# More result and row buffers for the expert tiles behind the last convolution, in the convolutions' room

## The chip, the core and the metric

The kernel runs on one core of a Trainium2 chip. The metric is the device time of one execution in microseconds (us). Before the change it is 3072.74 us, the median of ten runs (3070.18 to 3075.74).

The core's engines each work through their own list of instructions in order: PE (matrix products), ACT (activations and copies), DVE (elementwise work and reductions), POOL (GpSimd, which here issues the indirect DMAs too) and SP, which issues most of the other DMAs. Engines wait for each other through semaphores. In the profile, "idle before <- X" names what ended an idle time.

## The reference

A layer of 32 small convolution paths is followed by an attention layer without a softmax and a mixture of experts: each of the 25088 tokens goes to the two best of eight experts, and the weighted results are added to it.

```python
x = conv_paths(x)                    # 32 paths 256 -> 4 -> 3x3 -> 4 -> 256, summed, plus x
t = x.reshape(8, 3136, 256)
t = t + attn(layernorm(t))           # per head: q @ (k^T v / N), k and v normalised per head
t = t + moe(layernorm(t))
# moe(tokens), top 2 of 8 experts, weights normalised:
out = tokens
for e in range(8):
    h = gelu(tokens @ w1[e] + b1[e])
    out = out + combine[:, e:e+1] * (h @ w2[e] + b2[e])
```

## The kernel before

**Chunks and slots.** The tokens are cut into 56 chunks of 448 (`S = 56`, seven to an image). The loop over `s` (L1574) goes through 65 slots. In slot `s` the third convolution of chunk `s` is worked, with earlier steps of chunks `s + 1` and `s + 2`, the end of chunk `s - 1`, and attention and routing of chunk `s - 8`. Convolution work ends in slot 56. From slot 57 on (`S + 1`) only attention, routing and expert tiles are left; this is the tail, and the list `apart` is filled there, which makes some helpers choose other layouts (one PSUM bank for each half, an own `index` tile).

**Routing.** Once a chunk's two experts are known, POOL scatters its rows (`pay`, 259 numbers: 256 values, two weights and the token's number) into two DRAM tables, `regions`, by indirect DMA (L1191, eight for each chunk). `pay` has three buffers.

**Expert tiles.** Sorted rows are worked in 210 tiles of 256 rows (`N_ALL`), numbered in the order they are worked. `moe_steps` (L1505) is a hand-made pipeline of five steps for each tile number `n`:

- `tile_in(n)`: PE transposes the rows, ACT copies them to `eT`, DVE copies the token numbers to `index`
- `tile_mid(n - 1, ...)`: first product and GELU to `hT`, in two halves
- `take_rows(n + 2)` and `take_weights(n + 1)`: SP loads the 259 KB of rows and the 513 KB of the expert's weights
- `tile_out(n - 2, ...)`: second product; ACT scales the result by the gate into `y` (L1471), in two halves
- `tile_add()`: POOL adds one half of a finished `y` to the output in DRAM by indirect DMA (L1485)

Before the change `rows` has seven buffers, the weights `w` four and `y` four. A `y` buffer is free when the adds of the tile four back have landed.

**Order of the sums.** The two experts of a token must not be added at the same time. `ordered_sum` (L1493) therefore lets the adds of one block (a routing round `b` and a place `k` of the top two) wait until all adds of the block before have landed. Blocks begin at tiles 130, 137, 144, 149, 154, 158, 162, 165, 168, 172, 176 and 193, among others. The last round is known only when the last chunk is scattered; its tiles are 176 to 209.

**Who sets the order.** PE, ACT and DVE work in the order written out by hand (`places`, L614, and the sort in `issue`, L1536). POOL and SP take their DMAs in the order that the build gives. DMAs of POOL take turns on eight semaphores (lanes), and each one waits until the eighth before it has landed; SP's DMAs have lanes in the same way.

**Room.** `xtp`, `taps`, `split` and `hlp` (L95 to L98) hold the convolutions' tiles. They stay open to the end of the kernel, though nothing uses them in the tail.

Of the kernel before, what the change touches and what calls it, by code (L numbers as in the profile page):

```python
# [8 lines left out]
F32 = mybir.dt.float32  # L9
# [16 lines left out]
def kernel(  # L26
# [25 lines left out]
    B, N, C = x.shape  # L52
# [6 lines left out]
    P = 128  # L59
# [32 lines left out]
            tc.add_manual_dep(ins, halved[0].name, SYNC, reason="not needed by the first chunk")  # L92
        xs_in[s] = X

    xtp = ctx.enter_context(tc.tile_pool(name="xtp", bufs=4))  # L95
    taps = ctx.enter_context(tc.tile_pool(name="taps", bufs=1))
    split = ctx.enter_context(tc.tile_pool(name="split", bufs=1))
    hlp = ctx.enter_context(tc.tile_pool(name="hlp", bufs=2))  # L98
    setup_pool = tc.tile_pool(name="setup", bufs=1)
    setup = setup_pool.__enter__()  # L100

# [155 lines left out]
    def is_chunk(s):  # L257
        return 0 <= s < S
# [198 lines left out]
    slots = ctx.enter_context(tc.tile_pool(name="slots", bufs=4))  # L457
    work = ctx.enter_context(tc.tile_pool(name="work", bufs=2))
# [42 lines left out]
    ROW = C + 3  # L501
    WROW = 2 * NF * C + NF
# [101 lines left out]
    def unordered(ins, group, keep=()):  # L604

        tc.declare_no_dep(ins, group=group, keep=keep, reason="other rows")
# [85 lines left out]
    def conv3_steps(s):  # L692
        steps = []
        units = NF * NQ
        for step in range(0, 4 * units, 2):
            if is_chunk(s):
                steps.append((places["conv3"][0], lambda step=step: (pair(s, step), pair(s, step + 1))))
            if step == 0 and is_chunk(s - 1):
                steps.append((places["conv3"][1], lambda: sum_paths(s - 1, units - 1)))
            if step and step % 4 == 0 and is_chunk(s):  # L700
                steps.append((places["conv3"][1], lambda step=step: sum_paths(s, step // 4 - 1)))
        return steps
# [644 lines left out]
        return [(1.0, fn) for fn in (counts, runs, members, first_rows, experts, rest)]  # L1347


    got, weights_of, turned, hidden, ready = {}, {}, {}, {}, []  # L1350
    landed = set()

    def entry(i, j, most):

        place, own, k, partial, b = slot_of[i]
        loads, (value,) = nc.values_load_multi_w_load_instructions(
            place[0:1, j : j + 1], engines=[mybir.EngineType.SP],
            min_val=0, max_val=most,
            skip_runtime_bounds_check_because="a tile's row and expert, made on the chip",
        )  # L1360
        if b not in landed:
            landed.add(b)
            for ins in before[b]:
                tc.add_manual_dep(loads[0].ins, ins.name, SYNC, reason="rows of the tiles")
        return value
# [11 lines left out]

    def take_rows(i):
        row = entry(i, 0, E * CAPR - TR)
        z = slots.tile([P, 2, ROW], F32, tag="rows", name=f"rows_{i}", bufs=7)  # L1380
        region = regions[slot_of[i][2]]
        ins = nc.sync.dma_start(
            out=z, in_=region[bass.ds(row, TR), :].rearrange("(h p) c -> p h c", p=P)
        ).ins
        unordered(ins, "rows")
        tc.add_to_no_dep_group("tiles", ins)
        got[i] = z

    def take_weights(i):
        e = entry(i, 1, E - 1)  # L1390
        w = slots.tile([P, WROW], F32, tag="w", name=f"w_{i}")
        nc.sync.dma_start(
            out=w, in_=Wd[bass.ds(e, 1), :, :].rearrange("e p c -> (e p) c")
        )
        weights_of[i] = w
# [29 lines left out]
    apart = []  # L1425

    def bank_of(i, h, name):

        if h == 0:
            n = 1 if apart else 2  # L1430
            v = ps_mm.tile([P, n, 256], F32, tag="mm", name=f"{name}_{i}")
            hidden[i, name] = v
        elif apart:
            v = ps_mm.tile([P, 1, 256], F32, tag="mm", name=f"{name}_{i}_{h}")
        else:
            v = hidden[i, name]
        return v[:, h % v.shape[1], :]
# [17 lines left out]
    def tile_out(i, h):  # L1455
        w = weights_of[i]
        eT, g, _ = turned[i]
        if h == 0:
            hidden[i].append(work.tile([P, 2, C], F32, tag="y", name=f"y_{i}", bufs=4))
        hT, y = hidden[i]  # L1460
        own = slot_of[i][1]
        ps = bank_of(i, h, "py")
        nc.tensor.matmul(  # L1463
            ps, own.to_broadcast([P, P]), b2hl, start=True, stop=False
        )
        for f in range(NF):
            nc.tensor.matmul(  # L1467
                ps, hT[:, f, h * P : (h + 1) * P], w[:, (NF + f) * C : (NF + f + 1) * C],
                start=False, stop=(f == NF - 1),
            )  # L1470
        nc.scalar.activation(y[:, h, :], ps, AF.Identity, scale=g[:, h : h + 1])  # L1471
        ready.append((i, h))
# [53 lines left out]
    def at(name, steps):  # L1526

        out, last = [], 0.0
        for place, (_, fn) in zip(places[name], steps, strict=True):
            last = max(last, place)  # L1530
            out.append((last, last, [(0.0, fn)]))
        return out
# [32 lines left out]
    def put_off(m):  # L1565

        return m % NCH == NCH - 1 and m + 1 + A < S
# [6 lines left out]
    for s in range(S + A + 1):  # L1574
        a = s - A
        work_of = []
        era = " alone" if s < A else ""
        if s <= S:
            work_of.append((0.0, 1.0 if is_chunk(s) else 0.1, conv3_steps(s)))
        if is_chunk(s + 2):  # L1580
            work_of.extend(at("conv1" + era, conv1_steps(s + 2)))
        if is_chunk(s + 1):
            work_of.extend(at("taps" + era, [(0.0, lambda: spread_taps(s + 1))]))
            work_of.extend(at("conv2" + era, conv2_steps(s + 1)))
        if is_chunk(s - 1):
            if s < S:
                work_of.extend(at("end" + era, end_steps(s - 1)))
            else:
                work_of.append((0.12, 0.99, end_steps(s - 1)))
        if is_chunk(a + 1):  # L1590
            work_of.extend(at("fetch", [(0.0, lambda: fetch(a + 1))]))
        if is_chunk(a):
            opens = a % NCH == 0
            if opens:
                work_of.extend(at("image", image_steps(a // NCH)))
            if a + A > S:
                work_of.extend(at("attention first last" if opens else "attention last", attn_steps(a)))
            else:
                work_of.extend(at("attention first" if opens else "attention", attn_steps(a)))
        work_of.extend(left)  # L1600
        left = []
        group = waiting
        if waiting and put_off(waiting[0]):
            group = [] if waiting[0] == a - 1 else waiting[:1]
        if group and (len(group) == 2 or group[-1] % NCH == NCH - 1):
            last_image = group[-1] >= S - NCH
            compute, scatters = route_steps(group)
            rt = places["route" if s < S else "route last"]
            work_of.append((rt[0], rt[1], compute))
            if last_image:  # L1610
                work_of.append((places["scatter last"][0], 0.995, sum(scatters, [])))
            else:
                work_of.append((places["scatter"][0], 0.995, scatters[0]))
                left = [(0.0, places["scatter"][1], steps) for steps in scatters[1:]]
            if group[-1] in closing:
                work_of.append((places["plan"][0], places["plan"][1], plan_steps(closing.index(group[-1]))))
            waiting = waiting[len(group) :]
        while r + 1 < len(closing) and known_in[r + 1] <= s:
            r += 1
        if r >= 0 and r + 1 < len(closing):  # L1620
            goal = upto + (known_after[r] - 2 - upto) // (known_in[r + 1] - s)
            if r + 2 < len(closing):
                goal = min(known_after[r] - 2, goal if s < known_in[1] else tiles_by(s))
            work_of.append((places["tiles"][s <= known_in[r]], places["tiles"][2], moe_steps(upto, goal)))
            upto = goal
        if s == 1:
            center_router()
        if 1 <= s <= E:
            work_of.append((0.5, 0.5, [(0.0, lambda: copy_weights(s - 1))]))
            work_of.append((0.8, 0.8, [(0.0, lambda: empty_rows(s - 1))]))  # L1630
        if s == S + 1:
            apart.append(s)
        issue(*work_of)
        if is_chunk(a):
            waiting.append(a)
# [60 lines left out]
```

## Time and profile before

| what | value |
|---|---|
| median of ten runs | 3072.74 us |
| profiled execution | 3079.18 us |
| its span, first to last instruction | 3077.3 us |
| mean granted TensorE clock | 0.965 |
| PE busy over the span | 2850.1 us (93%) |
| POOL busy over the span | 1798.7 us (58%) |
| POOL, adds to the output (L1485), 420 of them | 408.1 us (258) and 250.9 us (162) |
| POOL, scatters (L1191), 448 of them | 428.1 us |

The shares of busy time are means over stages with different limits. The change acts in the last tenth of the span alone, so this part is read by itself. There the slices of 50 us show:

| slice (us) | PE busy | POOL busy | granted clock | DMA share |
|---|---|---|---|---|
| 2700 to 2750 | 45.43 | 34.27 | 0.93 | 1.01 |
| 2750 to 2800 | 39.10 | 37.92 | 0.83 | 0.84 |
| 2800 to 2850 | 45.00 | 36.57 | 0.93 | 0.95 |
| 2850 to 2900 | 39.77 | 37.59 | 0.86 | 0.83 |
| 2900 to 2950 | 44.59 | 30.21 | 0.97 | 0.92 |
| 2950 to 3000 | 47.48 | 41.76 | 1.00 | 0.95 |
| 3000 to 3050 | 50.00 | 39.23 | 1.00 | 0.94 |

"DMA share" is the mean busy share of the core's 16 DMA engines. POOL's busy time counts the making of an indirect DMA, not the 0.30 us between two of them, in which the next is issued.

### The profile page before, as it was taken

The page shows a single profiled execution, that of the slowest core. Times are in us where ns is not written, and L with a number is a line of the kernel's source. Part 1 is how long each engine was busy: PE and PEld are TensorE (multiplying, and loading weights), DVE is VectorE, ACT ScalarE, POOL GpSimd, SP SyncE. Part 2 cuts the span into 40 slices and gives each one's busy share as a digit, 9 for nine tenths or more (in the row PEclk, how much of TensorE's full clock was granted, in tenths as well). Part 3 has the DMA queues.
Part 4 walks back from the last instruction along what each step waited for, and adds up shares of the span by engine and source line. Part 5 has one row for each costly group of instructions (what it writes and reads, how often), then busy time and mean ns, then how long its engine had stood idle before and what let it go on. Part 6 is the DMA issues. An engine that isn't in the chain of part 4 may idle for free.

```text
span 3077.3 us, 54367 instructions
## 1 busy us (share of the span) xinstructions
PE 2850.1 (93%) x16901; PEld 1659.1 (54%) x16901; DVE 2144.8 (70%) x5705; ACT 1915.2 (62%) x3859; POOL 1798.7 (58%) x1333
## 2 busy tenths in 40 slices
PE   7999888888899999999999999999999997998898
PEld 3334444334455555555555555555555555787687
DVE  6877887888777877787877877787778775443100
ACT  4666566556566676667766766667666664554355
POOL 2332345444465766757666666676664656677677
PEclk9999899989899999999999999999999998998999
DMA  3555444436477777677777767778877766998897
GB/s 103 148 115 133 119 138 132 132 100 185 111 181 183 181 202 202 164 199 188 202 189 176 202 177 193 194 178 205 193 168 181 190 168 149 229 278 214 201 221 172
DMA packets 373233, 538.19 MB, mean 175 GB/s; under 512 B 91488, under 2 KB 283344, under 8 KB 372944
## 3 DMA queue, kind: packets, MB, share of 16 engines
q1 hardware_dynamic: 289984, 430.49, 48.7%
q0 software_dynamic: 82368, 103.47, 20.0%
q8 instruction: 135, 2.21, 0.3%
q14 instruction: 154, 1.26, 0.2%
q10 hardware_dynamic: 592, 0.76, 0.1%
HBM read 248.42 MB, written 192.75 MB: 143 GB/s over the span
## 4 chain that ended last, share of the span: by engine, by line
PE 54%; DVE 6%; DMA 4%; ACT 4%; POOL 3%; issue 3%; POOLq 0%; ACTq 0%; DVEq 0%; SPq 0%
PE ph L1447 11%; PE c L660 9%; PE py L1467 9%; PE su L681 8%; PE te L1403 3%; DMA out_dram<-y,index 3%; PE at L1010 2%; PE py L1463 2%; PE kv L837 2%; PE c L324 2%; DVE r L668 2%; ACT r L665 2%; POOL hsd L801 2%; PE at L1006 1%; PE c L288 1%
## 5 line engine op out<-in xcount | busy, mean ns | idle before, releaser
L668 DVE SCALAR_TENSOR_TENSOR r<-c,nb,r 128x448 f32<-128x448 f32 x1792 | 1127.2, 676 | 380.0 <-ACT r L665 375.3
L665 ACT ACTIVATE r<-c,b3t 128x448 f32<-128x448 f32 x1792 | 1036.9, 634 | 342.3 <-PE c L660 336.0
L660 PE MATMUL c<-hl,W3hl 64*128 64x448 f32 x3584 | 701.2, 430 | 36.1 <-ACT r L665 19.1
L1191 POOL DMA_INDIRECT regions<-pay,rrowi x448 | 428.1, 956 | 304.9 <-PE c L660 178.2
L660 PEld LDWEIGHTS c<-hl,W3hl 64*128 64x128 f32 x3584 | 331.9, 189 | 488.1 <-issue 216.6
L1485 POOL DMA_INDIRECT out_dram<-y,rows x258 | 408.1, 1582 | 319.4 <-ACT y L1471 241.5
L681 PE MATMUL su<-r,gather 128*32 128x448 f32 x3584 | 538.7, 565 | 44.3 <-DVE r L668 34.4
L1471 ACT ACTIVATE y<-py,rows 128x256 f32<-128x256 f32 x420 | 195.7, 473 | 467.4 <-PE py L1467 340.0
L1447 PE MATMUL ph<-eT,w 128*128 128x256 f32 x1680 | 458.5, 405 | 16.8 <-ACT hT L1451 7.9
L1467 PE MATMUL py<-w,hT 128*128 128x256 f32 x1680 | 434.9, 384 | 0.0
L1447 PEld LDWEIGHTS ph<-eT,w 128*128 128x128 f32 x1680 | 303.7, 197 | 147.0 <-ACT hT L1451 29.3
L801 POOL TENSOR_TENSOR hsd<-hsd,half 112x36 f32<-112x36 f32 x49 | 302.4, 6172 | 98.0 <-DVE hsd L799 95.2
L754 POOL TENSOR_TENSOR norm<-t,hmean 112x512 f32<-112x512 f32 x112 | 115.5, 1057 | 356.1 <-DVE hmean L743 242.8
L1467 PEld LDWEIGHTS py<-w,hT 128*128 128x128 f32 x1680 | 293.9, 193 | 27.1
L1485 POOL DMA_INDIRECT out_dram<-y,index x162 | 250.9, 1549 | 94.5 <-issue 27.1
L1451 ACT ACTIVATE hT<-ph,w 128x256 f32<-128x256 f32 x420 | 197.2, 478 | 166.6 <-PE ph L1447 111.5
L681 PEld LDWEIGHTS su<-r,gather 128*32 128x32 f32 x3584 | 99.1, 109 | 231.2 <-DVE r L668 105.8
L1463 PE MATMUL py<-b2hl,own 128*128 128x256 f32 x420 | 176.6, 421 | 17.3 <-ACT y L1471 8.3
L1015 DVE SCALAR_TENSOR_TENSOR X<-at,rs,X 112x256 f32<-112x256 f32 x224 | 106.7, 476 | 99.7 <-PE at L1010 98.8
L1463 PEld LDWEIGHTS py<-b2hl,own 128*128 128x128 f32 x420 | 80.8, 192 | 145.9 <-issue 49.1
L324 PE MATMUL c<-R,W2t 96*32 96x448 f32 x1344 | 152.3, 556 | 2.5 <-ACT r L665 2.4
L1403 PE MATMUL te<-ident,rows 128*128 128x128 f32 x840 | 136.3, 286 | 19.6 <-ACT y L1471 18.6
(267 smaller groups left out, 3282.6 us busy)
## 6 DMA issues: line engine op xcount, KB each, us to landing
w<-Wd SPq DMA_DIRECT2D x210, 513.0 KB
rows<-regions SPq DMA_DIRECT2D x210, 259.0 KB
xi<-in_x_dram SPq DMA_DIRECT2D x56, 448.0 KB
hl<-hi SPq DMA_DIRECT2D x112, 224.0 KB
tTs<-xT SPq DMA_DIRECT2D x56, 448.0 KB
ts<-t SPq DMA_DIRECT2D x56, 448.0 KB
tT<-tTs SPq DMA_DIRECT2D x56, 448.0 KB
X<-ts SPq DMA_DIRECT2D x56, 448.0 KB
```

Of the source, the lines that this page charges most:

```text
L324: nc.tensor.matmul(ps[0][32 * g : 32 * g + 32, :CH], W2t[:, g, dy, :], R[:, g, :].rearrange("q (r w) -> q r w", w=W58)[:, dy : dy + ROWS, ...
L660: product = nc.tensor.matmul(tiles[g][:, :CH], W3hl[rows, ab, cg, :], hl[rows, ab, :], start=True, stop=True)
L665: nc.scalar.activation(r, tiles[0][:, :CH], AF.Relu, bias=b3t[:, cg, 2 * ab : 2 * ab + 1])
L668: nc.vector.scalar_tensor_tensor(r, tiles[1][:, :CH], nb3[:, cg, 2 * ab + 1 : 2 * ab + 2], r, op0=ALU.max, op1=ALU.add,)
L681: nc.tensor.matmul(ps[32 * c4 : 32 * c4 + 32, :CH], gather, unit.pop((s, 4 * u + c4)), start=(ab == 0), stop=(ab == NQ - 1),)
L801: nc.gpsimd.tensor_tensor(sd, sd, half[:T, :].rearrange("q (k h) -> q k h", k=KT), ALU.pow)
L1191: ins = nc.gpsimd.indirect_dma_start(out=regions[n], out_offset=bass.IndirectOffsetOnAxis(ap=v["row_i"][:, (m - group[0]) * KT + k, n : n ...
L1403: nc.tensor.transpose(tp[:, f, h * P : (h + 1) * P], z[:, h, f * P : (f + 1) * P], ident)
L1447: nc.tensor.matmul(ps, w[:, f * C + hf * P : f * C + (hf + 1) * P], eT[:, f, :], start=(f == 0), stop=(f == NF - 1),)
L1463: nc.tensor.matmul(ps, own.to_broadcast([P, P]), b2hl, start=True, stop=False)
L1467: nc.tensor.matmul(ps, hT[:, f, h * P : (h + 1) * P], w[:, (NF + f) * C : (NF + f + 1) * C], start=False, stop=(f == NF - 1),)
L1485: ins = nc.gpsimd.indirect_dma_start(out=out_rows, out_offset=at, in_=y[:, h, :], in_offset=None, compute_op=ALU.add, **partial,).ins
```

## The change

The four pools of the convolutions are placed on the right side of SBUF and closed at slot `S + 1`; a pool `late` is opened in their room. A helper `buffer` chooses for each tile number, from slot 57 on, between the old buffers of a tag and the new ones, in a fixed turn: of twelve tiles in a row four take the old `y` buffers and eight the new ones; of eleven, seven take the old `rows` buffers and four the new. The weights go through the same helper with no new buffers. Nothing that is computed changes, nor what is loaded, scattered or added.

```diff
-    xtp = ctx.enter_context(tc.tile_pool(name="xtp", bufs=4))
-    taps = ctx.enter_context(tc.tile_pool(name="taps", bufs=1))
-    split = ctx.enter_context(tc.tile_pool(name="split", bufs=1))
-    hlp = ctx.enter_context(tc.tile_pool(name="hlp", bufs=2))
+    conv_pools = [
+        tc.tile_pool(name=name, bufs=bufs, side="right")
+        for name, bufs in (("xtp", 4), ("taps", 1), ("split", 1), ("hlp", 2))
+    ]
+    xtp, taps, split, hlp = (p.__enter__() for p in conv_pools)
...
+    more = {}
+    first_late = []
+
+    def buffer(i, pool, tag, bufs, shape):
+
+        if apart and not first_late:
+            first_late.append(i)
+        if apart and more[tag] and (i - first_late[0]) % (bufs + more[tag]) >= bufs:
+            return apart[0].tile(shape, F32, tag=tag, name=f"{tag}_{i}", bufs=more[tag])
+        return pool.tile(shape, F32, tag=tag, name=f"{tag}_{i}", bufs=bufs)
...
-        z = slots.tile([P, 2, ROW], F32, tag="rows", name=f"rows_{i}", bufs=7)
+        z = buffer(i, slots, "rows", 7, [P, 2, ROW])
...
-        w = slots.tile([P, WROW], F32, tag="w", name=f"w_{i}")
+        w = buffer(i, slots, "w", 4, [P, WROW])
...
-            hidden[i].append(work.tile([P, 2, C], F32, tag="y", name=f"y_{i}", bufs=4))
+            hidden[i].append(buffer(i, work, "y", 4, [P, 2, C]))
...
         if s == S + 1:
-            apart.append(s)
+            for pool in reversed(conv_pools):
+                pool.__exit__(None, None, None)
+            more.update(y=8, rows=4, w=0)
+            apart.append(
+                ctx.enter_context(tc.tile_pool(name="late", bufs=1, side="right"))
+            )
```

## The prediction, made before the changed kernel was run

> **What bounds the kernel now.** I read the waits by engine first. Up to 2714 us ACT never waits for a result buffer; from there to the end one wait leads all others on ACT. It is the wait for a `y` buffer, held until the adds of the tile four back have landed:
>
> ```profile
> ACT y L1471 <- DMA out_dram<-y,index: 116.8, 28, 11.6
> ```
>
> That looks like what the change is for. Second view: the timeline of POOL, which issues these adds (L1485) and the scatters of routed rows (L1191), each an indirect DMA.
>
> ```profile
> 2738.15 1.54 POOL L1485 DMA_INDIRECT out_dram<-y,index  x1 [0.30 <-issue]
> 2740.00 1.54 POOL L1485 DMA_INDIRECT out_dram<-y,index  x1 [0.30 <-ACT X L1053]
> 2749.34 1.54 POOL L1485 DMA_INDIRECT out_dram<-y,index  x1 [7.80 <-ACT lg L1019]
> 2751.19 1.54 POOL L1485 DMA_INDIRECT out_dram<-y,index  x1 [0.30 <-issue]
> 2753.03 1.54 POOL L1485 DMA_INDIRECT out_dram<-y,index  x1 [0.30 <-issue]
> 2754.88 1.54 POOL L1485 DMA_INDIRECT out_dram<-y,index  x1 [0.31 <-issue]
> 2756.73 0.97 POOL L1191 DMA_INDIRECT regions<-pay,rrowi  x1 [0.30 <-DVE rs L1025]
> 2758.01 0.96 POOL L1191 DMA_INDIRECT regions<-pay,rrowi  x1 [0.30 <-issue]
> ```
>
> An add takes 1.85 us of POOL (1.54 and 0.30 between), a scatter 1.25, back to back; it is so from 2688.36 to 3071.81, but for eight stops. The stop of 7.80 is put down to ACT, yet that `y` had long been written. Pairing ACT's `y` writes with POOL's adds in their order, tile 144, whose add opens here, was ready at 2736.11. The wait is the order of the sums: tile 144 is the first of a new block, and its add waits until all adds of the block before have landed. I call such a stop a drain.
>
> The same pairing over tiles 136 to 209 shows every half ready at least 0.53 us before its add starts (least at tile 207, 3060.49 against 3061.02), most 28.61 us before (tile 147). So POOL never waits for `y` in these 383 us: POOL is the bound, and PE and ACT wait for POOL. Its time is summed by the groups of POOL from 2689 on:
>
> ```profile
> L1485 POOL DMA_INDIRECT out_dram<-y,index x150 | 232.4, 1549 | 84.0 <-issue 26.5 <-ACT y L1471 21.9 <-ACT lg L1019 11.5
> L1191 POOL DMA_INDIRECT regions<-pay,rrowi x56 | 53.1, 948 | 17.1 <-issue 13.7 <-DMA regions<-pay,rrowi 1.2 <-DVE index L1413 0.6
> ```
>
> Busy 232.4 + 53.1 = 285.5, idle 84.0 + 17.1 = 101.1, together 386.6. Of the idle, 37.9 are the eight drains (7.80, 3.12, 4.74, 3.25, 6.52, 4.41, 4.88, 3.14), 3.15 the wait before tile 135 at 2688 (PE was late there), and 60 the 0.30 between 197 instructions. The change touches neither the busy time nor the 0.30. Only the drains are left to move.
>
> Third view: the stretches of the drains, whose last two columns are the share of the DMA engines and GB/s.
>
> ```profile
> 2741.60:2749.30 7.70, 7.70 (x46) 6.96 (x45) 3.22 (x18) 4.08 (x9) 0.00 (x0) 1.00 1.09 307
> 2787.80:2790.90 3.10, 3.10 (x12) 2.72 (x11) 0.81 (x2) 0.88 (x3) 0.00 (x1) 0.50 0.37 42
> 2809.20:2813.80 4.60, 4.60 (x40) 4.01 (x39) 1.65 (x12) 3.52 (x10) 0.00 (x0) 1.00 1.08 263
> 2884.80:2888.00 3.20, 3.20 (x11) 2.64 (x11) 0.50 (x4) 1.44 (x4) 0.00 (x0) 0.63 0.40 47
> 2898.80:2905.30 6.50, 6.36 (x34) 5.30 (x34) 0.34 (x2) 2.81 (x8) 0.00 (x1) 1.00 0.92 272
> 2919.80:2924.20 4.40, 4.40 (x26) 3.92 (x25) 0.30 (x2) 1.62 (x5) 0.01 (x1) 1.00 1.04 262
> 2938.70:2943.50 4.80, 4.80 (x27) 4.25 (x26) 0.23 (x2) 2.31 (x7) 0.00 (x0) 1.00 0.87 209
> 3006.10:3009.20 3.10, 3.10 (x20) 2.74 (x18) 0.30 (x2) 1.75 (x4) 0.00 (x1) 1.00 0.57 148
> ```
>
> A drain is as long as the adds take to land. With the DMA engines at 0.87 to 1.09 it lasts 4.4 to 7.8 us; at 0.37 and 0.40 it lasts 3.1 and 3.2. These two are quiet because PE had just stood still for a `y` buffer, and the weights, which come when PE has finished the tile four back, stood still with it. SP's timeline shows the pause:
>
> ```profile
> 2778.70 0.38 SPq L1382 DMA_DIRECT2D rows<-regions  x1
> ...
> 2786.02 0.47 ACT L1471 ACTIVATE y<-py,rows 128x256 f32<-128x256 f32 x1 [11.61 <-DMA out_dram<-y,index]
> ...
> 2791.96 0.33 SPq L1392 DMA_DIRECT2D w<-Wd  x1
> ```
>
> **The change part by part.** *Room and order.* Moving the four convolution pools to the other side changes addresses; the built program has the same instructions in the same order on all five engines. No wait differs before tile 127, and nothing can differ in time before 2714, where the first `y` wait ends late. Cost 0; no cover is needed.
>
> *Eight more `y` buffers.* A tile's `y` now waits for the adds of the tile twelve back. The 116.8 us of ACT's waits go, and with them most of the PE idle they make: in 50 us slices from 2700 to 3000 PE is idle 4.57 + 10.90 + 5.00 + 10.23 + 5.41 + 2.52 = 38.6 us. What is late next is POOL, with the same 206 instructions: gain on the path 0. PE runs up to twelve tiles ahead, until a later round's rows are not scattered yet (POOL's own scatters, last at 2876) or its work is done, and the last adds drain as now.
>
> PE ahead pulls loads forward: 513 KB of weights and 259 KB of rows a tile, for eight tiles 6.2 MB. At 286 GB/s (2700 to 2750) that is 22 us of DMA, where the three slices from 2700 to 2850 leave 150 - 50 x (1.01 + 0.84 + 0.95) = 10. So the engines stay full through the drain at 2787, and nothing pauses the loads at 2884. I price both at the mean of the five drains over 0.87: (7.80 + 4.74 + 6.52 + 4.41 + 4.88) / 5 = 5.67. That adds 5.67 - 3.12 + 5.67 - 3.25 = +5.0 us. The other six are taken as they are. Bounds for all eight: at 7.80 each 62.4 - 37.9 = +24.5; at 3.12 each 25.0 - 37.9 = -12.9, if the loads have gone ahead and leave the engines free.
>
> *Four more `rows` buffers.* From 2714 SP waits 10.5 us for ACT before issuing rows, six times; these waits go. Behind them in SP's queue stand the weights, which wait 156.7 us for PE by themselves, and PE waits nowhere for rows landing between 2700 and 3000. Cost 0, covered by the weights' wait; without that cover the rows come at most 10.5 us earlier, off POOL's path.
>
> *Waits that become explicit.* `pay` (L1046) waits for the scatters three chunks back, so far covered by the `y` waits; behind it on ACT stand `y`, `eT` and `hT`, and PE waits for these. At tile 153 it needs scatters issued by 2769; ACT was there at 2799 and would have to be over 20 us earlier to feel it. Were it felt, PE loses lead, not POOL: 0. POOL's lanes also wait for the eighth DMA back (10.6 us in the scatter stretches), and stay 0.30 apart throughout: 0, inside the upper bound if landings pass that.
>
> **Sum.** 0 + 5.0 + 0 + 0. The profiled execution took 3079.18 (span 3077.3), 6.4 above the median, so it would take 3084.2; on the median, 3072.74 + 5.0 = **3077.7 us**.
>
> The Trainium skill (Perfetto Trace Analysis, Optimization Strategy) says that consistent bubbles on the engine that should be saturated can mean too little SBUF for the next tile. The row above has such bubbles, 28 of them, but on ACT and PE, while POOL is the saturated one; by the rule the sum would be 3072.74 - 38.6 = 3034, by the row 3077.7. Against the change speaks DMA: Bandwidth & Descriptors (Issuing engines are not separate DMA queues): DMAs of all issuers run on the same 16 engines and interleave, as the drains' lengths against the engines' share agree.
>
> **The rivals.**
> *Slower.* Earlier loads keep the engines full from 2714 to 2850, and the landings there go to the longest seen: 2787 and 2809 last 7.80, 2884 and 3006 the loaded mean 5.67. 4.68 + 3.06 + 2.42 + 2.53 = +12.7, 3085.4. It decides once the eight drains gain 6.15 us together. For it: 1.09 at the 7.80 drain, and only 10 us of free DMA. Against it: the drain at 2809 lasted 4.74 at 1.08. Bound 3097.
> *Faster.* Loads are the same in number, so what comes early is missing later; drains fall to 3.12, -12.9, 3059.8. Against it: PE will still work its 4.13 us a tile through the late drains. A full gain of PE's idle (3034) would need POOL to wait for `y`, and it does not.
> *The change does nothing.* If the buffers never get ahead: 3072.7. Against it: the built program drops the waits.
>
> **How the numbers follow.** Within 0.2% (6.15 us, about what a measurement of this kernel can tell) hold the forecast (0.40) and the idle change (0.10): 0.50. Slower by more, the first rival and the forecast's upper side: 0.34. Faster by more: 0.16, of it 0.03 for the full gain. The drains' bounds give 3059.8 to 3097; I cut the upper end where about 0.06 is left: 3060 to 3090, below it 0.08.
>
> **What would show it.** Right: ACT's wait for `out_dram` almost gone, PE done tens of us before POOL, POOL's adds still 1.85 apart to the end, `y` ready long before its add, the drains at 2787 and 2884 with the engines near 1. Wrong: a POOL stop outside the block borders, drains that sum far from 43 us, or POOL clearly off 386.6 - 37.9 = 348.7 us outside them.

## The result, and the profile after

| | before | after |
|---|---|---|
| median of the runs of this comparison | 3073.62 us (28 runs) | 3084.06 us (8 runs) |
| ratio, 95% interval | | 1.0036, 1.0027 to 1.0045 |
| profiled execution / its span | 3079.18 / 3077.3 us | 3087.18 / 3085.2 us |
| mean granted TensorE clock | 0.965 | 0.963 |
| last matrix product of PE ends | 3066.6 us | 3040.7 us |
| from the start of tile 135's add to the end of the last add | 383.44 us | 393.39 us |

The kernel became 10.4 us slower. ACT and PE did what more result buffers are for: ACT's wait for `y`, 116.8 us before, is almost gone, and PE is done 25.9 us earlier than before. The waits by engine, from 2714 us on (us in total, times, longest); ACT first, then PE:

```profile
ACT y L1483 <- DMA out_dram<-y,index: 6.2, 6, 2.4
```

```profile
PE te L1415 <- DMA rows<-regions: 25.9, 1, 25.9
```

The second row is PE's lead running out once, up to 2857 us: it has run up to tiles whose rows POOL has not yet scattered. POOL did not become faster. The groups of POOL from 2686 us on (busy us, mean ns of one, idle before):

```profile
L1497 POOL DMA_INDIRECT out_dram<-y,index x150 | 232.4, 1550 | 92.2 <-ACT y L1483 27.2 <-issue 22.6 <-ACT hT L1463 15.8
L1192 POOL DMA_INDIRECT regions<-pay,rrowi x56 | 54.9, 980 | 17.1 <-issue 15.5 <-DMA regions<-pay,rrowi 0.6 <-DVE full_i L1255 0.3
```

The adds (now L1497) are as many and as long as before, the scatters (L1192) cost 1.8 us more. What grew is the idle time before the adds, 84.0 to 92.2, though an add's `y` now lies ready far earlier. POOL's timeline shows where, at the first of the eight drains (start, length, and in brackets the idle time before):

```profile
2736.05 1.54 POOL L1497 DMA_INDIRECT out_dram<-y,index  x1 [0.30 <-ACT eT L1419]
2737.89 1.54 POOL L1497 DMA_INDIRECT out_dram<-y,index  x1 [0.30 <-ACT hT L1463]
2746.20 1.54 POOL L1497 DMA_INDIRECT out_dram<-y,index  x1 [6.76 <-DVE X L1016]
2748.05 1.54 POOL L1497 DMA_INDIRECT out_dram<-y,index  x1 [0.30 <-ACT hT L1463]
```

Taken from the start of tile 135's add, the 393.39 us are 287.31 busy, 60.09 in the 0.30 between instructions, and 46.00 in eight drains; before it was 285.52, 60.07 and 37.86. There is no other stop of POOL in either. Of the 9.95 us, 8.14 lie in the drains and 1.79 in POOL's own instructions. (The profiled executions differ by 8.00 us, since the one of after came to tile 135 some 2 us earlier, where nothing can differ yet.) The drains one by one, by the tile that opens the block:

| tile | 144 | 149 | 154 | 165 | 168 | 172 | 176 | 193 | sum |
|---|---|---|---|---|---|---|---|---|---|
| before | 7.80 | 3.12 | 4.74 | 3.25 | 6.52 | 4.41 | 4.88 | 3.14 | 37.86 |
| after | 6.76 | 4.86 | 5.45 | 5.47 | 5.09 | 7.08 | 6.18 | 5.11 | 46.00 |

The stretches of the after kernel's drains (length; busy time and count on PE, its weight loads, DVE, ACT and POOL; clock; share of the DMA engines, the packets' times added up, which can pass 1; GB/s):

```profile
2739.40:2746.20 6.80, 6.80 (x43) 6.15 (x42) 2.32 (x9) 3.68 (x9) 0.04 (x2) 1.00 1.07 281
2784.70:2789.50 4.80, 4.80 (x42) 4.36 (x40) 2.06 (x14) 2.98 (x8) 0.00 (x0) 1.00 1.08 290
2807.70:2813.10 5.40, 1.86 (x17) 1.38 (x16) 4.29 (x26) 3.77 (x10) 0.04 (x1) 1.00 1.00 264
2885.90:2891.30 5.40, 5.40 (x32) 4.79 (x31) 0.17 (x1) 3.23 (x8) 0.00 (x0) 1.00 0.92 259
2902.10:2907.20 5.10, 5.10 (x29) 4.49 (x28) 0.30 (x2) 2.95 (x7) 0.02 (x1) 1.00 1.04 267
2921.70:2928.80 7.10, 7.10 (x40) 6.30 (x39) 0.60 (x4) 4.43 (x9) 0.03 (x1) 1.00 0.94 254
2943.30:2949.40 6.10, 6.10 (x35) 5.40 (x34) 0.30 (x2) 3.94 (x8) 0.00 (x0) 1.00 0.89 256
3012.00:3017.10 5.10, 5.10 (x28) 4.53 (x28) 0.30 (x2) 3.08 (x7) 0.02 (x1) 1.00 0.69 223
```

No drain is quiet any more: where two of the eight had the DMA engines at 0.37 and 0.40, now the least is 0.69, and the least length is 4.86 us.

### The profile page after: what moved, and what is told of

The parts are those of the page before. It is cut to its first block, busy times and chain, and to the rows that moved or that the text cites. A ratio compares the mean times of both kernels' runs of the same rounds, so it can differ in the third digit from the quotient of the medians.

```text
span 3085.2 us, 54340 instructions
## 1 busy us (share of the span) xinstructions
PE 2828.6 (92%) x16901; PEld 1643.4 (53%) x16901; DVE 2144.6 (70%) x5705; ACT 1928.4 (63%) x3859; POOL 1800.9 (58%) x1333
## 4 chain that ended last, share of the span: by engine, by line
PE 44%; DVE 4%; ACT 2%; POOL 2%; issue 2%; DMA 2%; POOLq 0%; SPq 0%; ACTq 0%; DVEq 0%
PE ph L1459 10%; PE py L1479 9%; PE c L661 6%; PE su L682 6%; PE te L1415 3%; PE py L1475 2%; PE at L1011 2%; PE c L325 2%; PE kv L838 2%; DVE r L669 1%; ACT r L666 1%; PE at L1007 1%; PE c L289 1%; POOL hsd L802 1%; PE tu L729 1%
## 5 line engine op out<-in xcount | busy, mean ns | idle before, releaser
L1192 POOL DMA_INDIRECT regions<-pay,rrowi x448 | 429.9, 960 | 302.2 <-PE c L661 182.1
L1497 POOL DMA_INDIRECT out_dram<-y,rows x258 | 408.0, 1581 | 318.4 <-ACT y L1483 244.4
L1459 PE MATMUL ph<-eT,w 128*128 128x256 f32 x1680 | 449.8, 399 | 19.4 <-ACT hT L1463 8.0
L1497 POOL DMA_INDIRECT out_dram<-y,index x162 | 250.9, 1549 | 103.8 <-ACT y L1483 30.8
L1415 PE MATMUL te<-ident,rows 128*128 128x128 f32 x840 | 134.3, 283 | 26.9 <-DMA rows<-regions 25.9
L1419 ACT COPY eT<-te 128x512 f32<-128x512 f32 x210 | 123.5, 588 | 48.0 <-PE te L1415 45.7
```

What stands on the lines that cost most here:

```text
L1192: ins = nc.gpsimd.indirect_dma_start(out=regions[n], out_offset=bass.IndirectOffsetOnAxis(ap=v["row_i"][:, (m - group[0]) * KT + k, n : n ...
L1415: nc.tensor.transpose(tp[:, f, h * P : (h + 1) * P], z[:, h, f * P : (f + 1) * P], ident)
L1459: nc.tensor.matmul(ps, w[:, f * C + hf * P : f * C + (hf + 1) * P], eT[:, f, :], start=(f == 0), stop=(f == NF - 1),)
L1497: ins = nc.gpsimd.indirect_dma_start(out=out_rows, out_offset=at, in_=y[:, h, :], in_offset=None, compute_op=ALU.add, **partial,).ins
```

## The experiments

Ten more kernels were run, on three chips. "Length" is the same stretch as above, from tile 135's add to the last; it comes from one profiled execution, the ratio from all runs. Each run's ratio is against the kernel before on its own chip. "Drains" are POOL's waits over 0.31 us at block borders. One execution speaks for its kernel only within some us: e7_quiet10 is 6.8 us longer than before by its length, 12.9 by its ratio, and e4_no_weights and e5_hold8 were profiled in the slowest of all their executions.

| run | median us | ratio, 95% interval | length us | drains us |
|---|---|---|---|---|
| before | 3073.62 | | 383.44 | 37.86 |
| after | 3084.06 | 1.0036, 1.0027 to 1.0045 | 393.39 | 46.00 |
| e1_rows_only | 3075.36 | 1.0001, 0.9992 to 1.0010 | 383.15 | 36.51 |
| e2_y_only | 3084.85 | 1.0032, 1.0020 to 1.0044 | 393.02 | 46.43 |
| e4_no_weights | 3068.64 | 0.9982, 0.9972 to 0.9991 | 379.70 | 32.99 |
| e5_hold8 | 3080.56 | 1.0013, 1.0004 to 1.0022 | 391.04 | 45.44 |
| e7_quiet10 | 3086.21 | 1.0042, 1.0028 to 1.0056 | 390.27 | 43.96 |
| e11_quiet_old_y | 3088.16 | 1.0044, 1.0031 to 1.0058 | 395.26 | 42.58 |
| e15_quiet_end | 3073.60 | 0.9997, 0.9988 to 1.0006 | 379.62 | 33.35 |
| e13_cover | 3065.68 | 0.9967, 0.9958 to 0.9976 | 376.34 | 29.87 |
| e14_cover_old_y | 3065.33 | 0.9971, 0.9962 to 0.9980 | 376.37 | 29.42 |
| e16_cover_quiet | 3061.53 | 0.9959, 0.9945 to 0.9972 | 370.23 | 24.02 |

**Which buffers?** The change was made in halves: the pools moved with the four `rows` buffers alone, and with the eight `y` buffers alone.

```diff
-            more.update(y=8, rows=4, w=0)
+            more.update(y=0, rows=4, w=0)     # e1_rows_only
+            more.update(y=8, rows=0, w=0)     # e2_y_only
```

> The changed kernel with no new y buffers (four, as before), the moved pools and the four new rows buffers kept. Theory (POOL is the bound from 2688 us on; y buffers let PE run ahead, its loads then run through the drains and lengthen them): ACT's waits for out_dram are back, the two quiet drains too, drains sum near 38 us, time 3073.6 within 4 us. Rival (the rows buffers or the new addresses cost the time): 3084 or near it.

> The changed kernel with the eight new y buffers and no new rows buffers. Theory: drains sum near 46 us as in the changed kernel, time 3084 within 4 us. Rival (the rows buffers cost it): 3074.

The rows buffers and the new places of the pools cost nothing that can be measured; the `y` buffers alone make the whole slowdown, and their drains (46.43) are those of the full change (46.00). Single drains differ more: before tile 149 it is 6.78 us here and 4.86 in after, before tile 193 it is 2.10 and 5.11.

**Is it the weights' traffic?** From tile 140 on every tile uses the weights of tile 139: 70 loads of 513 KB less.

```diff
     def take_weights(i):
+        if i >= 140:
+            weights_of[i] = weights_of[i - 1]
+            return
         e = entry(i, 1, E - 1)
```

> The changed kernel, but from tile 140 on the weights are not loaded: all later tiles use those of tile 139, so 70 loads of 513 KB are left out. Theory (the drains are long because loads run beside the adds): DMA share falls, the eight drains fall to 3 to 4 us each, 24 to 32 in sum against 46.0, POOL's adds stay 1.85 us apart: time 3084 - 14 to - 22, so 3062 to 3070. Rival (drains are set by POOL or by the adds themselves, the loads are innocent): drains stay 5 to 7, time 3082 to 3085. Second rival (POOL is not the bound, DMA bandwidth is): far below 3062, since a third of the tail's bytes is gone.

The drains fall by 13 us, to 32.99, and the kernel is faster than before: the eight buffers do no harm once most of the loads' traffic is gone. It is a little more than expected, since the `rows` loads (259 KB a tile) stay and some still lie in the drains: the one before tile 165 took 5.88 us with 1.2 MB of loads in it, the one before 154, with none in it, 3.11.

**Is it how many loads there are, or where they lie?** Three attempts to place them failed, and say why. In the first the weight load of tile `i` waits until the second add of tile `i - 8` has landed, which takes PE's lead away again. The main part of the edit (`added` holds the second add of each tile issued so far):

```diff
-        nc.sync.dma_start(
+        ins = nc.sync.dma_start(
             out=w, in_=Wd[bass.ds(e, 1), :, :].rearrange("e p c -> (e p) c")
-        )
+        ).ins
+        if apart and i - 8 in added:
+            tc.add_manual_dep(ins, added[i - 8].name, SYNC, reason="loads keep to the adds")
```

> The changed kernel with one wait added: SP issues the weights of a tile only when the second add of the tile eight back has landed, so loads keep pace with POOL, while the y buffers stay twelve. Theory: PE's lead shrinks, loads pause in the drains as they did before the change, drains sum 34 to 42 us, time 3070 to 3080. Rival (the new buffers themselves cost time, through addresses or the other waits): 3084 as with the change.

This was a miss: the drains are 45.44 us and the time lies 0.6 us above its 3080. Over all runs part of the loss is back (ratio 1.0013 against 1.0036, and the intervals lie apart), so PE's lead may have a share in it. Yet in the profiled execution PE ends at 3069.9 us, as late as before, and the drains are as long as with the lead: the lack of a lead alone does not make them short. The loads here are let go by adds that land, and adds land in the drains: SP issues eleven weight loads within the eight drains, against six before the change. Two of them, and the end of the drain they lie in (which began at 2737.45):

```profile
2742.28 0.34 SPq L1405 DMA_DIRECT2D w<-Wd  x1
2744.48 0.33 SPq L1405 DMA_DIRECT2D w<-Wd  x1
...
2745.39 1.54 POOL L1500 DMA_INDIRECT out_dram<-y,index  x1 [7.94 <-ACT lg L1020]
```

The next two hold the loads from the drains: where the tile waited for is the last or last but one of its block, the load waits for the first tile of the next block.

```diff
+        j = i - 10                            # e7; i - 8 in e11, with no new buffers
+        for n in (1, 2):
+            if j in added and place_of(j) != place_of(j + n):
+                j += n
+                break
+        if apart and j in added:
+            tc.add_manual_dep(ins, added[j].name, SYNC, reason="loads keep out of a drain")
```

> The new buffers stay; the weight load of tile i waits for the second add of tile i - 10, and where that tile is the last or last but one of its block, for the first tile of the next block, so that no load is let go in a drain. Theory (a drain is long because weight loads are in flight beside the landing adds, whoever lets them go): the eight drains sum to 25 to 33 us, as in the run without the loads (33.0), and the time is 3064 to 3072. Rival (PE's own pace or the number of bytes in the stage makes the landings long, wherever the loads lie): the drains stay at 42 or more and the time at 3079 or more.

> No new buffers at all (as before), but the loads held back as in the run above, by the tile eight back, since PE is never further ahead with four result buffers. Theory of the drains: they sum to 25 to 33 us against 37.9 before and the time is 3063 to 3070, faster than before without a new buffer. Rival (PE has no slack with the old buffers, a held load makes POOL wait outside the block borders): the drains fall but stops over 0.6 us elsewhere give it back, 3071 to 3080. Rival (the phase of the loads is of no account): drains 36 to 40, 3071 to 3077.

Both missed. In e7_quiet10 the edit did not do what it was to do. Three of its drains, with the columns as above:

```profile
2785.20:2788.20 3.00, 0.00 (x0) 0.00 (x0) 0.00 (x0) 0.00 (x0) 0.04 (x1) 0.50 0.36 44
2883.40:2889.60 6.20, 6.20 (x24) 5.20 (x24) 4.21 (x12) 2.53 (x6) 0.00 (x1) 0.69 0.74 191
2900.50:2907.60 7.10, 7.10 (x29) 6.00 (x30) 0.34 (x2) 2.68 (x6) 0.00 (x0) 0.76 0.91 277
```

Only the first is free of loads. Three loads wait for the same tile. In the block that opens at 2889.6 its adds have landed some 6 us later; the loads and the rows behind them are 3 x (513 + 259) KB = 2.3 MB, at the 277 GB/s of the third row 8.4 us, and a block of three or four tiles is 11 to 15 us long (1.85 us an add): they run into the next drain. SP's timeline before the third drain shows the loads going out in a row:

```profile
2895.51 0.33 SPq L1408 DMA_DIRECT2D w<-Wd  x1
...
2897.36 0.33 SPq L1408 DMA_DIRECT2D w<-Wd  x1
...
2899.46 0.33 SPq L1408 DMA_DIRECT2D w<-Wd  x1
2900.38 0.39 SPq L1398 DMA_DIRECT2D rows<-regions  x1
```

In e11_quiet_old_y the drains did not fall either (42.58 us, before the change 37.86), and with no lead to spare the held loads made PE late: POOL now waits outside the block borders for `y`, 11.74 us in all. The first rival named these waits, but with shorter drains:

```profile
2979.65 1.54 POOL L1508 DMA_INDIRECT out_dram<-y,index  x1 [0.30 <-issue]
2981.91 1.54 POOL L1508 DMA_INDIRECT out_dram<-y,index  x1 [0.72 <-ACT y L1494]
2983.76 1.54 POOL L1508 DMA_INDIRECT out_dram<-y,index  x1 [0.31 <-issue]
2986.04 1.54 POOL L1508 DMA_INDIRECT out_dram<-y,index  x1 [0.74 <-ACT y L1494]
```

So the loads were let go right at a drain's end instead: where the tile ten back is one of the last three of its block, the load waits for the last add of that block.

```diff
-        for n in (1, 2):
+        for n in (1, 2, 3):
             if j in added and place_of(j) != place_of(j + n):
-                j += n
+                j += n - 1
                 break
```

> The new buffers stay; where the tile ten back is one of the last three of its block, the weight load waits for the last add of that block, so it is let go as the drain ends (in the run that waited for the first tile of the next block three loads were let go some 8 us later and ran into the next drain, only the drain before tile 149 was free of loads: 3.01 us). Theory (loads in flight beside the landing adds make a drain long, and the place of the loads decides): with most loads worked off in the first 8 to 10 us of a block, most of the eight drains show less than 500 KB of loads and take 3 to 4 us, 24 to 33 us in sum, and the time is 3062 to 3071. Rival (a drain is as long as the number of loads in the stage makes it, wherever they lie): the sum stays over 40 us and the time over 3078.

The stretches of its eight drains:

```profile
2740.90:2748.00 7.10, 7.10 (x43) 6.47 (x43) 2.72 (x8) 3.29 (x10) 0.03 (x1) 1.00 0.78 199
2786.50:2789.60 3.10, 0.00 (x0) 0.00 (x0) 0.00 (x0) 0.00 (x0) 0.00 (x0) 0.50 0.37 42
2807.80:2812.80 5.00, 5.00 (x30) 4.49 (x29) 2.03 (x8) 2.54 (x6) 0.00 (x0) 1.00 0.76 182
2884.40:2887.40 3.00, 0.00 (x0) 0.00 (x0) 0.00 (x0) 0.25 (x1) 0.00 (x1) 0.82 0.34 44
2898.20:2901.60 3.40, 3.40 (x21) 3.01 (x19) 0.17 (x1) 2.09 (x5) 0.00 (x1) 1.00 0.50 69
2916.10:2919.40 3.30, 3.30 (x19) 2.91 (x19) 0.30 (x2) 2.16 (x5) 0.00 (x0) 1.00 0.51 75
2933.90:2937.50 3.60, 3.60 (x21) 3.19 (x20) 0.30 (x2) 2.12 (x5) 0.04 (x1) 1.00 0.61 94
3000.10:3004.80 4.70, 4.70 (x27) 4.18 (x26) 0.30 (x2) 2.96 (x6) 0.00 (x0) 1.00 0.34 112
```

Five drains are now 3.0 to 3.6 us, with the DMA engines moving 42 to 94 GB/s. In three of these five PE is busy from end to end at clock 1.00, so it is not PE's work that makes a drain long. The other three still have loads in them and take 4.7 to 7.1. With every byte loaded that the after kernel loads, and the same buffers, the median is 10.5 us lower, and the intervals of the two ratios lie apart. So the place of the loads decides, but the edit reaches only five of eight: the time, 3073.60, is 2.6 us above what was expected, and the sum of 33.35 just above its 33. The loss of the change is won back, no more: against the kernel before the ratio is 0.9997, and its interval holds 1. The DMA view of the drain before tile 172, in after (2921 to 2929 us) and then in this run (2916 to 2920), by queue (packets, MB, share of the 16 engines); q1 carries SP's loads, q0 POOL's adds:

```profile
q1 hardware_dynamic: 868, 1.66, 69.4%
q0 software_dynamic: 326, 0.29, 27.2%
```

```profile
q0 software_dynamic: 262, 0.23, 41.9%
q1 hardware_dynamic: 60, 0.10, 14.7%
```

In the first the loads take 69.4% of the engines' time while the adds of a few hundred KB wait to land. (The second window reaches past the drain at both ends; in the drain itself the loads' share is 0.03.) From the packets of the nine kernels without moved scatters, I worked out the share of the engines that the loads' queue had in each drain before tiles 144 to 176, 63 drains. In 13 it is under 0.10: they take 3.00 to 3.61 us (mean 3.21). In the other 50, where it is 0.22 or more, they take 3.92 to 7.94. The two sets do not overlap. The drain before tile 193 is left out and does not follow this: with the loads at 0.34 to 0.69 of the engines it takes 2.10 to 5.11 us in eight of the nine kernels, and without any 2.13 in e4_no_weights. The adds of tiles 191 and 192, which end there, move 8 bytes a row in all nine, where full ones move 1024. So the rule is shown only where adds with data must land beside the loads.

**Can POOL work in a drain?** Eleven scatters of the last chunks are kept back and put, by an order on POOL without a wait, between the last add of a block and the first of the next: four before tile 149, three before 154, one before 165, three before 168. The main part of the edit (`let_go` issues up to the given number of the scatters kept back):

```diff
+        moved = []
+        if apart and h == 0 and slot_of[i][2::2] != slot_of[i - 1][2::2]:
+            moved = let_go(COVER)             # COVER = 4: the scatters kept back
+            for m in moved:
+                tc.add_manual_dep(m, last_add[0].name, NOSYNC, reason="in the drain")
...
         ordered_sum(ins, slot_of[i][4], slot_of[i][2])
+        for m in moved:
+            tc.add_manual_dep(ins, m.name, NOSYNC, reason="in the drain")
+        last_add[:] = [ins]
```

> The new buffers stay; eleven scatters of the last chunks are held back and issued by POOL between the last add of a block and the first of the next: four before tile 149, three before 154, one before 165, three before 168. Theory (the drain is a fixed wait for landings, POOL can work in it): the visible waits there fall by 1.25 us for each scatter, by 4.5 + 3.75 + 1.25 + 3.6 = 13 us together, to a time of 3069 to 3074. Rival (a scatter put into the drain makes the landings late by as much as it hides, or a later stage waits for the held rows): less than 5 us is saved, 3079 or more.

> No new buffers at all (as before), with the same eleven scatters moved to the block borders. Theory: the drains there were 3.1, 4.7, 3.3 and 6.5 us before, so 3.1 + 3.75 + 1.25 + 3.75 = 11.9 us goes, 3060 to 3064, faster than before by more than the new buffers could give. Rival (held rows or a held payload buffer makes DVE, PE or the last round late): a stop of over 0.6 us outside the borders, 3070 or more.

POOL's timeline of e13_cover at the border before tile 154, where the after kernel stood still for 5.45 us:

```profile
2795.53 1.54 POOL L1526 DMA_INDIRECT out_dram<-y,index  x1 [0.30 <-issue]
2797.38 0.97 POOL L1213 DMA_INDIRECT regions<-pay,rrowi  x1 [0.30 <-issue]
2798.66 0.96 POOL L1213 DMA_INDIRECT regions<-pay,rrowi  x1 [0.30 <-DMA out_dram<-y,index]
2799.92 0.94 POOL L1213 DMA_INDIRECT regions<-pay,rrowi  x1 [0.30 <-DVE index L1449]
2801.17 1.59 POOL L1526 DMA_INDIRECT out_dram<-y,index  x1 [0.30 <-issue]
```

The drain has vanished behind three scatters that POOL had to issue anyway. The kernel before has three such borders already, before tiles 137, 158 and 162: six, six and five scatters stand there between the two adds, and the wait left is 0.30 us. The one before tile 158, with its first and last scatter:

```profile
2835.63 1.59 POOL L1485 DMA_INDIRECT out_dram<-y,index  x1 [0.31 <-issue]
2837.52 0.95 POOL L1191 DMA_INDIRECT regions<-pay,rrowi  x1 [0.30 <-issue]
...
2843.76 0.94 POOL L1191 DMA_INDIRECT regions<-pay,rrowi  x1 [0.30 <-issue]
2845.01 1.59 POOL L1485 DMA_INDIRECT out_dram<-y,index  x1 [0.30 <-issue]
```

In e13_cover the waits left before 149, 154, 165 and 168 are 1.65, 0.30, 3.61 and 1.79 us, against 20.87 in after: 13.5 us less, for 13 expected. From the last add of a block to the first of the next these four borders last 21.6 us, scatters included, so the landings did not come later by as much as the scatters hide, as the rival had it. The time, 3065.68, is below the 3069 to 3074 expected; the drains before 144, 172 and 193 were shorter too, by 3.5 us together, which the moved scatters don't explain. With the buffers of before (e14_cover_old_y) the same edit gives 3065.33, 1.3 us outside its 3060 to 3064. No stop came up outside the borders; at the border before tile 158 one of 1.12 us did in e13_cover, where five scatters are left of the six. The ratios of the two are alike: beside this edit the new `y` buffers are neither gain nor loss. That they are no loss here, though they were 10 us alone, is not explained by a run.

**Both together.** The loads let go at the drains' ends, and the scatters in the drains.

> The eleven held-back scatters of the cover run (drains in sight 29.9 us in sum) and the loads let go at the drains' ends, with the new buffers. Theory: the five drains that the scatters leave in sight (before 144, 165, 172, 176, 193: 6.1, 3.6, 6.3, 6.3 and 3.0 us) fall to about 3, 2, 3, 3 and 2 us and those before 149, 154 and 168 to about 0.3, so some 14 us remain and the time is 3048 to 3056, the fastest of all. Rival (the place of the loads is of no account): 3063 to 3069, as with the cover alone.

3061.53 us, the lowest of all, 12.8 us below the kernel before on its chip. It is not the 3048 to 3056 expected: 24.02 us of drains are left, not 14. Three of the five in sight still have 0.6 to 1.3 MB of loads in them (6.11, 4.18 and 5.39 us before 144, 165 and 172). Its interval overlaps that of the cover alone, so what the placing of loads adds to it is not settled.

## Why the prediction was right, and where it was off

**The bound: right.** POOL is the bound, PE and ACT only wait for it. ACT's 116.8 us of waits went but for 6.2, PE ended 25.9 us earlier, and not a microsecond of it reached the end. The Trainium skill's sentence on consistent bubbles (Perfetto Trace Analysis, Optimization Strategy) speaks of the engine that should be saturated, and here that was POOL: put to PE's bubbles, which were real, it gave 3034, and the measured time is 50 us above that. e2_y_only shows it without the other parts.

**Room, rows buffers: right.** Priced at 0; e1_rows_only measured a ratio of 1.0001.

**The waits that become explicit: right.** POOL outside the drains takes 345.6 us before and 347.4 after from tile 135 on, and never stops outside a block's border. The 1.8 us are scatters, five of which took 1.29 to 1.36 us instead of 0.95 around 2864 to 2876. POOL's busy time in this stretch lies between 285.5 and 287.3 us over all the kernels run, so it isn't shown that the change makes them.

**The drains: right in kind, too small in size.** The measured 3084.06 lies inside 3060 to 3090, but the forecast of 3077.7 is 6.4 us low, and its class, no change beyond 0.2%, which had the best chance (0.50), did not come. What the prediction says of PE pulling loads forward into the two quiet drains happened: 4.86 and 5.47 us, for the 5.67 priced. That is +3.96 of the +5.0. The step that failed is "The other six are taken as they are": together they gained 4.18 us (-1.04, +0.71, -1.43, +2.67, +1.30 and +1.97). In e2_y_only the split is 5.92 and 2.65, so single drains differ between like kernels, by up to 3 us, but in neither do the six stay as they were. Four of the six rose, though they had loads in them before. It may be that a PE that no longer pauses shifts the loads against every drain; no run shows what sets a loaded drain's length between 3.9 and 7.9 us. The mean of loaded drains, 5.67, was at hand: at that price for all eight, 8 x 5.67 - 37.9 = +7.5 us stands against the +8.1 measured, a nearness seen only afterwards. With the 1.8 of the scatters that makes the 9.95 of the profiles, and 10.4 by the medians.

**The rivals.** The slower one (+12.7 us) named the same mechanism and the right side of its point of 6.15 us, with the wrong places: it put the drains at 2787 and 2809 at 7.80 us each, which measured 4.86 and 5.45. Its size was nearer than the forecast's. The faster one, that loads which come early would be missing later, fell: the least late drain is 5.09 us. The loads do run out earlier, at 3031.7 us instead of 3056.5, but the last drain has ended at 3017 by then. Its cause, that a drain without loads lasts 3.1 us, holds, and was had by placing the loads, not by running ahead.

**What the prediction read too simply.** "A drain is as long as the adds take to land" leaves out about 1 us: from the signal that the last add has landed to the start of the next pass 0.78 to 1.10 us in all 72 drains of the nine kernels, quiet or loaded. And the eighth row of its drains, 3.10 us at a share of 0.57, fits neither of its two groups; it is the one before tile 193, whose adds have next to nothing to land.

**The rule on shared engines** (the Trainium skill, DMA: Bandwidth & Descriptors, Issuing engines are not separate DMA queues) stands: DMAs of all issuers share 16 engines, and the 63 drains show its price here, 3.2 us alone against 3.9 to 7.9 with SP's loads. Whether the engines' turns or the memory behind them set that price, no run tells apart.

## What to carry to other kernels

A wait that leads the list of waits may sit on an engine that is only being paced; find the engine without idle time in the stage first, and ask what the paced engine will do to the bound one once it runs free. Where the bound engine must wait for its own transfers to land, the loads of others that lie in that moment lengthen it, so place them after it: that shortened the drains as much as leaving 70 of them out (33.35 and 32.99 us). Holding them by the landing of any earlier add still lets some go inside that moment. Better still, give the waiting engine work that it has to do anyway: eleven moved instructions won about 10 us where eight buffers had lost as much.

## What the runs showed of the hardware

An indirect add of 128 rows that is alone lands 2.7 us after its start, whether it moves 1024 bytes a row (the first half of tile 206 in the after kernel: 2.70) or 8 (the last five there: 2.68 to 2.72). Without loads, but with other adds in flight, it takes up to 3.85 us (same trace, from 3035 us on). With loads beside them the last four before a drain landed after 5.65 to 6.81 us (2936 to 2943 us of the same trace).

A quiet drain does not end when the engines go idle: in e15_quiet_end the last packet of the adds before tile 172 ends at 2918.04 us, the landing is signalled at 2918.37, and the next add starts at 2919.47. So some 3 us of a drain (3.00 to 3.61 in the 13 quiet ones) could not be had by moving loads at all, only by covering it.
